# A masked row LSTM on one core: another deal of the input channels and gates, 32 products of 64 rows a half-step instead of 33, in an order of its own

## The chip, the cores and the metric

The kernel runs on one core of a Trainium2 chip. The time is that of the device for one execution, in microseconds (us), and less is better. The core has four engines that matter here: TensorE (PE) multiplies, and its weight loads are shown apart as PEld; VectorE (DVE), ScalarE (ACT) and GpSimd (POOL) work elementwise, and GpSimd sees only SBUF, not the PSUM banks into which TensorE writes. SyncE (SP) issues the DMAs. Each engine takes its instructions in the order of the program and waits on semaphores for the others.

## What is computed

The input x is 8 images of 96 channels, 128 rows and 128 pixels. It is normalised in 32 groups of channels. A convolution along the row (input to state, "is", three taps, masked) gives 384 gate channels for every pixel, and then a recurrence runs down the 128 rows. At each row a second convolution along the row (state to state, "ss", three taps) is taken of the last hidden row h, the two are added, and four gates f, i, o, g update the cell c and h. The sum of x and h is the output.

```python
m = np.ones((c_out, c_in, 1, kw), dtype=np.float32)
m[:, :, :, cx + 1:] = 0.0
m[:, :, 0, cx] = 0.0
m[:co, :ci, 0, cx] = 1.0
m[co:2 * co, :2 * ci, 0, cx] = 1.0
m[2 * co:3 * co, :, 0, cx] = 1.0
...
ss = lax.conv_general_dilated(h, W_ss, window_strides=(1,), padding=((1, 1),), dimension_numbers=('NCW', 'OIW', 'NCW')) + b_ss[None, :, None]
gates = ss + row_in
g5 = gates.reshape(B, 3, 4, Oc, Wd)
f = jax.nn.sigmoid(g5[:, :, 0].reshape(B, O, Wd))
i = jax.nn.sigmoid(g5[:, :, 1].reshape(B, O, Wd))
o = jax.nn.sigmoid(g5[:, :, 2].reshape(B, O, Wd))
g = jnp.tanh(g5[:, :, 3].reshape(B, O, Wd))
c_new = f * c + i * g
h_new = o * jnp.tanh(c_new)
```

The mask: the tap on the right is zero; the tap on the left is whole; of the centre tap the first third of the gate channels of each kind sees the first third of the input channels, the second third two thirds of them, and the last third sees all. All arithmetic is in fp32.

## The kernel before

**Tiles.** The 384 gate channels are three tiles of 128: A, B and C. Each is one PSUM bank of 128 x 512, in which the first 256 columns ("half 0") are for the even pixels and the last 256 for the odd ones ("half 1"), 4 images x 64 pixels each. A tile holds 96 channels of one gate (A: f, B: i, C: o) and 32 of g. The 8 images are two halves of 4 (s = 0, 1), whose recurrences are independent; they take turns. One row of one half is a **half-step** n, so there are 256, and place(n) tells the row and the half.

**Products.** The three taps of a pair of pixels are computed from four combinations (vs, the sum of the even and odd inputs; vf, their difference; vd, two shifted differences), with weights combined to match. A product is called by the weight it uses: "1" (vs, half 0), "2" (vf, half 1), "0" (vd, half 0), "3" (vd, half 1). Its 128 rows are 96 channels of h and 32 channels of x, which ride along in the same operand (normalise_shared puts x there). The other 64 channels of x have their own operands xs, of three parts, each held twice on rows 0 to 63 and 64 to 127, and products P, Q and E of 64 rows (half 0, half 1, half 0).

**Lanes.** The 128 rows of TensorE are used as two lanes of 64 rows, which run at once. In the regular part every product of 128 rows is issued as two of 64, one on each lane; P, Q and E need one lane only. In the order string a mark tells the lane: "<" rows 0 to 63, ">" rows 64 to 127; the second half of a product always takes the lane that the first didn't. That makes 24 products of 64 rows for h and 9 for xs, 33 a half-step. Two lanes must not write one bank at the same time, so HalfStep.mm keeps the last writer of each bank and, when the lane changes, has TensorE wait for its end (lines 489 to 491):

```python
before = self.writer.get(a)
if before is not None and before[0] != rows and whole not in (before[0], rows):
    lanes.wait(before[1])
```

lanes.wait drops a wait if one for the same or a later product has been made. The record of a bank's last writer is dropped at "even" below, when VectorE takes over.

**One half-step**, for a tile: products 1, 2, P and Q; "copy" (cp, ScalarE, L563) takes half 0 to SBUF with the bias; "even" (lo, VectorE, L567) adds copy and half 1 into half 0; "odd" (hi, L571) their difference into half 1; then products 0, 3 and E are added on top. Then tanh (ta, L575) and sigmoid (si, L587) on ScalarE, forget (fg, L592), gated (gt; the even pixels on GpSimd, L599, the odd ones on VectorE, L601), cell (ce, L611), cell_tanh (th, L616), output (ou, L624), which writes h into the operand tile hx of the next row. From hx come the sum (S, L637) and the difference (F, L641) on VectorE and the shifted differences (D, L645) on GpSimd. The residual (re, L662) adds h to x in place, and the rows are stored.

**Order.** The order of the engines' work in the regular part is written out by hand in the string PERIOD, which do(n, PERIOD, by_lanes=True) issues for every half-step n from 2 on. A name is an operation and a tile; a quote mark puts it to the half-step before (two marks, two before), "+" to the next, "*" to the one after; "a" and "b" are the even and odd pixels, "l" and "h" the first and last two images. W1, W2, W3 (widen, add_pixels, subtract_pixels: the xs of an image four rows ahead) and U (normalise_shared) are GpSimd's, X is the same on ScalarE. S, F and D are of the half-step two later than the name says. Before:

```python
PERIOD = (
    "1B> 3C'< D'' 2A> 0C'< 1A> siBa' 2B< 3C'> 1B< EC'> 2C< taA' 0C'> re'' 1C< fg' taB' PB+> "
    "PC+< cpA W1 loA cpB 1C> hiA loB hiB siBb' QCl+< taCa' taCb' EA< 2C> gtb' W2 3A< siC' "
    "0B> gta' 0A< cpC 3B> QA+< W3 cea' tha' EB> PA+< ceb' loC 0A> 0B< oua' thb' oub' X F' "
    "3A< 3B> QB*> S' 2A+< 2B+> 1A+< U QCh+> siA hiC"
)
```

**Other names.** hold() has a GpSimd instruction wait for a VectorE one that reads two SBUF operands: the shifted difference for the sum or difference before it, and the first of GpSimd's W or U after a residual for that residual. finish(n) and work(n) issue the loads (load, load_rows) and stores on SP's queue. In the first 150 us the statistics of the normalisation are taken while x streams in through the ring of buffers, first_rows copies the first rows out of PSUM, and the first half-steps run beside it, from the table of events. LAST is the order of the final half-steps.

Of the kernel before, what the change touches and what calls it, by code (L numbers as in the profile page):

```python
# [21 lines left out]
def kernel(  # L22
# [51 lines left out]
    O4 = 4 * C  # L74
    wl = const.tile([P, w.shape[1]], F32, name="wl")
# [3 lines left out]
    wh = const.tile([P, O4], F32, name="wh")  # L79
# [8 lines left out]
    wo = [wx[:, 0, :], wx[:, 1, :], tap[3]]  # L88

    def load_weights():  # L90
        nc.gpsimd.memset(pick, 0.0)
        nc.sync.dma_start(wl, w)
        for j in range(3):
            for lo, hi, shift in ((0, C, 0), (C, P, 2)):
                cols = slice(lo + (j + shift) % 3, hi, 3)
                nc.vector.tensor_scalar(
                    pick[:, j, cols], gm[:, 0, cols], quarter_of[:, j : j + 1], None, ALU.mult
                )
        for t in range(2):
            for half in range(2):  # L100
                nc.scalar.activation(
                    wt2[half * C2 : (half + 1) * C2, t], w_own[t * C2 : (t + 1) * C2], AF.Identity
                )

    def make_weights():

        for a in range(3):
            for j in range(4):
                third = a if j == 3 else j
                cols = bass.ds(a * P + j * 32, 32)  # L110
                if third < 2:
                    nc.gpsimd.memset(tap[0][C:P, cols], 0.0)
                if third < 1:
                    for h in range(2):
                        nc.gpsimd.memset(tap[4][h * C2 + 32 : (h + 1) * C2, cols], 0.0)
        nc.gpsimd.tensor_add(wm[:, 2, :], tap[1], tap[2])
# [6 lines left out]
        nc.gpsimd.tensor_scalar_mul(wh, tap[3], 0.5)  # L123
# [17 lines left out]
    cs = [const.tile([C, 2, BH, J], F32, tag=f"c{s}", name=f"c{s}") for s in range(NH)]  # L141
    for s in range(NH):
        nc.gpsimd.memset(xw[s][:, :, J : J + 1], 0.0)
        nc.gpsimd.memset(hx[s][0][0:C, 0], 0.0)
        for i in range(2):
            nc.gpsimd.memset(hx[s][i][:, :, 0, :, J : J + 1], 0.0)
            nc.gpsimd.memset(hx[s][i][:, :, 1, :, 0:1], 0.0)
# [9 lines left out]
    def load_rows(s, k, lo=0, hi=R):  # L157
        src = rows_of(s, k, 0, C2, lo, hi)
# [44 lines left out]
    def first_rows(b):  # L203
# [3 lines left out]
        for i in range(2):  # L207
            nc.scalar.activation(xr[s][i * C2 : (i + 1) * C2, j], first[b][0:C2], AF.Identity)
# [126 lines left out]
    def add_pixels(xw, n, total, engine=nc.gpsimd):  # L335

        engine.tensor_add(total, xw[:, 0:n, 0:J], xw[:, 0:n, J + 1 :])  # L337

    def subtract_pixels(xw, n, differences, engine=nc.gpsimd):

        engine.tensor_sub(  # L341
            differences,
            strided(xw[:, 0, :], 0, [(W + 1, n), (J, 2), (1, J)]),
            strided(xw[:, 0, :], J + 1, [(W + 1, n), (0, 2), (1, J)]),
# [13 lines left out]
    def own_row(xw, s, r, lo=0, hi=BH, engine=nc.gpsimd):  # L358
# [8 lines left out]
        )  # L367

# [25 lines left out]
    order = {"A": 0, "B": 1, "C": 2}  # L394

    def gt(n, s, row, shape=(C, 2 * HB)):
# [6 lines left out]
        "0": (0, 0, ("vd", 1)),  # L403
        "3": (1, 3, ("vd", 0)),
# [48 lines left out]
    residuals = []  # L453
# [3 lines left out]
    class HalfStep:  # L457


        def __init__(self, n):  # L460
            self.n, (self.row, self.s) = n, place(n)
            self.ps, self.m1, self.moving, self.done, self.gates, self.th = {}, {}, {}, set(), None, None
            self.started, self.images, self.halves, self.writer = set(), {}, {}, {}
            self.even_input = self.last = None
            self.hx = hx[self.s][self.row // R % 2][:, self.row % R]
            self.xs = xs[self.s][self.row // R % 2][:, self.row % R]
# [35 lines left out]
        def own(self, a, i):  # L502

            low = a == order["A"] or (a == order["C"] and (self.s == 0 or (self.n, i) == (1, 2)))
            rhs = self.xs[:, i].rearrange("p b j -> p (b j)")
            self.mm(a, i % 2, wo[i], rhs, slice(0, C2) if low else slice(C2, P))
# [24 lines left out]
        def t_(self, a):  # L531
# [5 lines left out]
            for half in range(2):  # L537
                self.mm(a, half, wh, rhs, rows)
# [34 lines left out]
        def tanh(self, a, lo=0, hi=BH, t=None):  # L573
            g, ps = self.g[a * 32 : (a + 1) * 32], self.ps[a][C:P]
            nc.scalar.activation(self.part(g, lo, hi, t), self.part(ps, lo, hi, t), AF.Tanh)  # L575


        def sigmoid(self, a, lo=0, hi=BH, t=None):
            if self.row == 0 and a == 0:
                return  # L580
            gate = self.part(self.ps[a][0:C], lo, hi, t)
            if t == 0 and NH < self.n < last:
# [4 lines left out]
            nc.scalar.activation(to, gate, AF.Sigmoid)  # L587

# [5 lines left out]
        def gated(self, lo=0, hi=BH, t=None):  # L594
            to = self.g if self.row > 0 else self.c
            to, i, g = (self.part(ap, lo, hi, t) for ap in (to, self.ps[1][0:C], self.g))
            if t == 0 and self.even_input is not None:
                i = self.even_input.rearrange("p (b j) -> p b j", b=BH)
                nc.gpsimd.tensor_mul(to, i, g)  # L599
# [34 lines left out]

        def total(self, engine=nc.vector, lo=0, hi=BH):
            e, o = self.pair(lo, hi)
            self.last = engine.tensor_add(self.operand("vs")[:, 0, lo:hi], e, o)  # L637

        def difference(self, engine=nc.vector, lo=0, hi=BH):
            e, o = self.pair(lo, hi)  # L640
            self.last = engine.tensor_sub(self.operand("vf")[:, 0, lo:hi], o, e)  # L641

        def shifted(self, lo=0, hi=BH):
            h = self.hx[:, 0, lo, :]
            diff = nc.gpsimd.tensor_sub(  # L645
                self.operand("vd", 2)[:, :, lo:hi],
                strided(h, 1, [(BH * JP - 1, 2), (JP, hi - lo), (1, J)]),
                strided(h, 0, [(BH * JP + 1, 2), (JP, hi - lo), (1, J)]),
            )
            hold(diff, self.last)  # L650

        def residual(self, lo=0, hi=BH, t=None):
# [8 lines left out]
            else:  # L661
                residuals.append(nc.vector.tensor_add(xo, xo, self.h))  # L662
# [28 lines left out]
    def beside(s, k, *images):  # L691
# [4 lines left out]
        (shared(0, 1, 0), own(0, 1, 3), [(load_rows, 0, 2)]),  # L696
# [3 lines left out]
        (shared(1, 1, 3), own(1, 1, 3), [(load_rows, 1, 2), (load, 0, 2)]),  # L700
# [5 lines left out]
    def work(n):  # L706
# [3 lines left out]
        if n < len(FIRST):  # L710
# [13 lines left out]
    def prepare(n, which="123"):  # L724
# [14 lines left out]
        for part, *args in now:  # L739
            made = part(*args)  # L740
            if made is not None and made.ins.engine == E.Pool and residuals:
                hold(made, residuals[-1])
                residuals.clear()
# [3 lines left out]
    def finish(n):  # L747
# [14 lines left out]
        "1B> 3C'< D'' 2A> 0C'< 1A> siBa' 2B< 3C'> 1B< EC'> 2C< taA' 0C'> re'' 1C< fg' taB' PB+> "  # L762
        "PC+< cpA W1 loA cpB 1C> hiA loB hiB siBb' QCl+< taCa' taCb' EA< 2C> gtb' W2 3A< siC' "
        "0B> gta' 0A< cpC 3B> QA+< W3 cea' tha' EB> PA+< ceb' loC 0A> 0B< oua' thb' oub' X F' "
        "3A< 3B> QB*> S' 2A+< 2B+> 1A+< U QCh+> siA hiC"
    )
    LAST = (
        "0C'' 3C'' EC'' siBa'' taA'' re''' taB'' taCa'' gta'' PB taCb'' siBb'' QC QB fg'' PA "
        "gtb'' cea'' QA PC siC'' tha'' ceb'' oua'' thb'' oub'' EA EB EC F'' S'' D'' re'' 1A "
        "2A 1B 1C 2B 2C cpA loA hiA cpB loB 3A hiB 0A 0B 3B cpC loC hiC 0C 3C taA siA fg taB "  # L770
        "siBa siBb taCa taCb gta gtb siC ceb cea thb tha oub oua rea reb"
# [17 lines left out]
    def do(n, names, by_lanes=False):  # L789

        for name in names.split():
# [22 lines left out]
            if part in ("S", "F", "D"):  # L814
# [21 lines left out]
        [x_pool.tile([P, CH], F32, tag=f"x{s}", name=f"xs{s}") for s in range(NH)]  # L836
        + [const.tile([P, CH], F32, tag=f"piece{i}", name=f"piece{i}") for i in range(2)]
        + [
            xs[s][1].rearrange("p r t b j -> p (r t b j)")[:, 0:CH]
            for s in range(NH)  # L840
        ]
    )
# [8 lines left out]
    def next_row():  # L851
        late[0].scale()
        late[0].shift()
        for j in range(BH - 1):
# [9 lines left out]
    def operands(n):  # L864
# [5 lines left out]
        step.done |= {"S", "F", "D"}  # L870
# [39 lines left out]
    def keep_warm(count):  # L910
        if not early_done and 1 not in steps:
# [31 lines left out]
            do(-2, "PA PB QA QB PC QC EA EB EC"),  # L943
# [16 lines left out]
        at(5, 7): lambda: (  # L960
            do(-2, "loA hiA"),
# [11 lines left out]
            do(-2, "taA"),  # L973
# [3 lines left out]
            do(-2, "taB"),  # L977
# [7 lines left out]
            do(-2, "siC"),  # L985
# [234 lines left out]
```

## Time and profile before

| | |
|---|---|
| time, median of 3 runs | 1965.98 us (1965.78 to 1966.8) |
| span of the profiled execution, first to last instruction | 1965.0 us |
| mean granted TensorE clock | 0.995 |
| chain of waits, TensorE's share | 94%, of which the products of line 492 93% |
| mean DMA rate | 119 GB/s |
| start, 0 to 150 us: PE, DVE, ACT busy | 92.84, 110.27, 99.64 us |
| end, 1940 to 1965 us: PE, DVE busy | 16.38, 16.11 us |

The profile shows one execution. A row of a timeline has the start and the duration in us, the engine, the line of the kernel, the operation, the output and inputs by name, partitions x elements, and in brackets how long the engine had been idle and what ended it; neighbours of one kind are drawn together ("x2"). The groups give busy time, mean duration in ns, and the idle time before them. One matmul instruction of fp32 shows as two records, its two passes. Engines off the chain may be idle without cost.

### The profile page before, as it was taken

Reading aid. Unit: us, or ns where it says so; the run is one execution under the profiler, and the core shown is the slowest. Engines: PE = TensorE matmul, PEld = TensorE weight load, DVE = VectorE, ACT = ScalarE, POOL = GpSimd, SP = SyncE. Lnnn points to the kernel's source line nnn. Section 1 sums busy time; section 2 is a strip of 40 time slices with the busy share of each in tenths; the row PEclk is TensorE's granted clock in tenths of the full one; section 3 lists DMA queues with packets and bytes.
Section 4 is the critical chain, followed back from the end, with each engine's and each line's share of the span. In section 5 each row is a group of like instructions: output and inputs, shape, how many; then the busy total and the mean of one; then the engine's idle time right before and its main releaser. Section 6 shows DMA issues by size and latency. Waiting matters only on the chain.

```text
span 1965.0 us, 46105 instructions
## 1 busy us (share of the span) xinstructions
PE 1899.2 (97%) x17416; PEld 1817.2 (92%) x17416; DVE 1798.8 (92%) x4015; ACT 1558.1 (79%) x3493; POOL 1354.2 (69%) x1645
## 2 busy tenths in 40 slices
PE   3689999999999999999999999999999999999998
PEld 0359999999999999999999999999999999999997
DVE  5888999999999999999999999999999999999997
ACT  6678788878888887887888788888888878888886
POOL 3347777777777777777777777777777777777751
PEclk9989999999999999999999999999999999999999
DMA  9994434544443454445345453534544443354411
GB/s 402 408 309 94 102 81 115 119 98 101 100 107 85 106 119 98 109 91 115 86 98 119 98 117 87 116 88 91 119 106 111 93 107 96 83 119 112 104 33 33
DMA packets 101277, 234.64 MB, mean 119 GB/s; under 512 B 5824, under 2 KB 7360, under 8 KB 95040
## 3 DMA queue, kind: packets, MB, share of 16 engines
q1 hardware_dynamic: 101056, 231.70, 45.8%
q8 instruction: 138, 2.26, 0.5%
q14 instruction: 83, 0.68, 0.1%
HBM read 181.34 MB, written 50.33 MB: 118 GB/s over the span
## 4 chain that ended last, share of the span: by engine, by line
PE 94%; DMA 3%; DVE 2%; ACT 1%; issue 0%; POOL 0%; SPq 0%; DVEq 0%; ACTq 0%
PE ps L492 93%; DMA xs<-in_x_dram 3%; DVE bst L1098 1%; PE pv L274 0%; PE rows L198 0%; ACT g L575 0%; PE rows L183 0%; ACT xs L239 0%; ACT ps L587 0%; SPq L1085 0%; DVE hx L624 0%; POOL xw L320 0%; PE dm L274 0%; ACT xs L240 0%; ACT L587 0%
## 5 line engine op out<-in xcount | busy, mean ns | idle before, releaser
L492 PE MATMUL ps<-vd,wl 64*128 64x256 f32 (+1 forms) x6080 | 1190.4, 376 | 2.8 <-DVE ps L571 2.7
L492 PEld LDWEIGHTS ps<-vd,wl 64*128 64x128 f32 (+1 forms) x6080 | 871.1, 186 | 21.9 <-issue 3.5
L492 PE MATMUL ps<-vs,wm 64*128 64x256 f32 (+1 forms) x3046 | 821.5, 377 | 0.7 <-DVE vs L637 0.7
L492 PE MATMUL ps<-vf,wm 64*128 64x256 f32 (+1 forms) x3046 | 765.5, 377 | 0.0
L492 PE MATMUL ps<-xs,wx 64*128 64x128 f32 (+1 forms) x3582 | 747.7, 349 | 1.8 <-POOL xs L337 1.7
L492 PEld LDWEIGHTS ps<-xs,wx 64*128 64x128 f32 x3582 | 605.7, 188 | 7.1 <-POOL xs L337 3.3
L587 ACT ACTIVATE ps<-ps 96x512 f32<-96x512 f32 (+1 forms) x768 | 388.2, 506 | 232.3 <-PE ps L492 223.8
L492 PEld LDWEIGHTS ps<-vs,wm 64*128 64x128 f32 (+1 forms) x3046 | 529.3, 187 | 12.6 <-issue 1.6
L575 ACT ACTIVATE g<-ps 32x256 f32<-32x256 f32 (+1 forms) x1021 | 468.2, 481 | 19.3 <-PE ps L492 0.6
L492 PEld LDWEIGHTS ps<-vf,wm 64*128 64x128 f32 (+1 forms) x3046 | 461.9, 186 | 18.1 <-DVE vf L641 1.0
L492 PE MATMUL ps<-xs,wt 64*128 64x256 f32 x1518 | 449.3, 377 | 0.0
L563 ACT ACTIVATE m<-ps,wl 128x256 f32<-128x256 f32 x766 | 362.3, 473 | 106.6 <-PE ps L492 81.4
L645 POOL TENSOR_TENSOR vd<-hx 128x512 f32<-128x512 f32 x257 | 288.0, 1121 | 179.9 <-DVE vs L637 171.8
L567 DVE TENSOR_TENSOR ps<-m,ps 128x256 f32<-128x256 f32 x768 | 324.1, 422 | 79.4 <-ACT m L563 79.2
L571 DVE TENSOR_TENSOR ps<-m,ps 128x256 f32<-128x256 f32 x768 | 327.4, 427 | 17.7
L662 DVE TENSOR_TENSOR x<-x,hx 96x512 f32<-96x512 f32 x253 | 339.3, 1341 | 0.0
L320 POOL TENSOR_SCALAR xw<-xr,rstd,nmr 128x512 f32<-128x512 f32 (+1 forms) x267 | 209.2, 785 | 131.7 <-DVE x L662 114.1
L320 POOL TENSOR_SCALAR hx<-x,rstd,nmr 32x512 f32<-32x512 f32 (+1 forms) x245 | 219.4, 895 | 75.2 <-POOL xs L341 53.6
L341 POOL TENSOR_TENSOR xs<-xw 128x512 f32<-128x512 f32 (+1 forms) x254 | 269.8, 1062 | 0.0
L492 PEld LDWEIGHTS ps<-xs,wt 64*128 64x128 f32 x1518 | 264.8, 187 | 0.9 <-issue 0.3
L599 POOL TENSOR_TENSOR g<-i,g 96x256 f32<-96x256 f32 x251 | 181.9, 725 | 120.6 <-ACT g L575 112.7
L616 ACT ACTIVATE th<-c 96x256 f32<-96x256 f32 (+1 forms) x509 | 191.0, 418 | 2.4 <-DVE c L611 2.1
(101 smaller groups left out, 1487.4 us busy)
## 6 DMA issues: line engine op xcount, KB each, us to landing
xr<-in_x_dram SPq DMA_DIRECT2D x124, 512.0 KB, 6.9
x<-in_x_dram SPq DMA_DIRECT2D x62, 768.0 KB, 8.6
out_dram<-x SPq DMA_DIRECT2D x62, 768.0 KB, 5.0
xs<-in_x_dram SPq DMA_DIRECT2D x31, 1024.0 KB, 10.8
piece<-in_x_dram SPq DMA_DIRECT2D x16, 1024.0 KB, 11.0
x<-in_x_dram SPq DMA_DIRECT2D x62, 256.0 KB, 6.3
out_dram<-x SPq DMA_DIRECT2D x2, 576.0 KB, 3.7
xs<-in_x_dram SPq DMA_DIRECT2D x2, 512.0 KB, 9.7
```

The source lines that it names most:

```text
L320: return engine.tensor_scalar(dst, src, scale, shift, ALU.mult, ALU.add)
L341: engine.tensor_sub(differences, strided(xw[:, 0, :], 0, [(W + 1, n), (J, 2), (1, J)]), strided(xw[:, 0, :], J + 1, [(W + 1, n), (0, 2), ( ...
L492: made = nc.tensor.matmul(self.ps[a][:, bass.ts(half, HB)][:, cols], weights[rows, bass.ts(a, P)], rhs[rows, cols], start=new, stop=False, ...
L563: nc.scalar.activation(self.m1[a], m1, AF.Identity, bias=column)
L567: nc.vector.tensor_add(self.ps[a][:, 0:HB], self.m1[a], self.ps[a][:, HB:])
L571: nc.vector.tensor_sub(hi, self.m1[a], hi)
L575: nc.scalar.activation(self.part(g, lo, hi, t), self.part(ps, lo, hi, t), AF.Tanh)
L587: nc.scalar.activation(to, gate, AF.Sigmoid)
L599: nc.gpsimd.tensor_mul(to, i, g)
L616: nc.scalar.activation(self.part(self.th, lo, hi, t), self.part(self.c, lo, hi, t), AF.Tanh)
L645: diff = nc.gpsimd.tensor_sub(self.operand("vd", 2)[:, :, lo:hi], strided(h, 1, [(BH * JP - 1, 2), (JP, hi - lo), (1, J)]), strided(h, 0, ...
L662: residuals.append(nc.vector.tensor_add(xo, xo, self.h))
```

## The change

The gate channels are dealt to the tiles by the thirds of the mask. A holds f and the last third of o; B holds i and the last third of g; C holds the first two thirds of o and of g. The 32 channels of x that ride along with h are now the first third, and xs holds the other two. With this deal tile C, whose gates are of the first two thirds only, needs of the third part of xs only the 32 channels of the second third; these ride on rows 96 to 127 of a new operand te (called ve in the products), in the product "3". So product E of tile C goes: 32 products of 64 rows. Q is whole, no longer in two halves, and E writes half 1.

The shifted difference splits: shifted_even (D0) writes te's first 96 rows, shifted_odd (D1) the operand vo of 128 rows. Rows 96 to 127 of te are a copy of rows 64 to 95 of xs's third part, made by a DMA, spare, on SP's queue, and at the start by ScalarE (spare_rows). The last third of the output gate is a sigmoid of its own (o2), from A's bank to C's. Tile A has no tanh any more. GpSimd is held behind sums and differences as well as residuals, whichever GpSimd instruction comes next (after_reads). first_rows copies in four pieces instead of two; the ring has other buffers; the order strings are new.

```diff
-    wh = const.tile([P, O4], F32, name="wh")
+    wh = const.tile([P, 2, 2 * P], F32, name="wh")
...
-    wo = [wx[:, 0, :], wx[:, 1, :], tap[3]]
+    wo = [wx[:, 0, :], wx[:, 1, :], tap[4]]
...
+    te = [const.tile([P, 2, R, BH * J], F32, tag=f"te{s}", name=f"te{s}") for s in range(NH)]
...
-        src = rows_of(s, k, 0, C2, lo, hi)
+        src = rows_of(s, k, 32, C, lo, hi)
...
-        nc.sync.dma_start(flat[C:P], rows_of(s, k, C2, C))
+        nc.sync.dma_start(flat[C:P], rows_of(s, k, 0, 32))
...
-        for i in range(2):
-            nc.scalar.activation(xr[s][i * C2 : (i + 1) * C2, j], first[b][0:C2], AF.Identity)
+        for i in range(4):
+            of = 32 + i % 2 * 32
+            nc.scalar.activation(
+                xr[s][i * 32 : (i + 1) * 32, j], first[b][of : of + 32], AF.Identity
+            )
...
+    def spare_of(s, i, r0, r1, lo=0, hi=BH):
+
+        return (
+            te[s][C:P, i, r0:r1].rearrange("p r (b j) -> p r b j", b=BH)[:, :, lo:hi],
+            xs[s][i][C2 : C2 + 32, r0:r1, 2, lo:hi],
+        )
...
+    def spare(s, k, r0=0, r1=R):
+        nc.sync.dma_start(*spare_of(s, k % 2, r0, r1))
...
-        "0": (0, 0, ("vd", 1)),
-        "3": (1, 3, ("vd", 0)),
+        "0": (0, 0, ("vo", 0)),
+        "3": (1, 3, ("ve", 0)),
...
+    def after_reads(made):
+
+        if both_sbuf and made is not None and made.ins.engine == E.Pool:
+            hold(made, both_sbuf[-1])
+            both_sbuf.clear()
...
-                self.mm(a, i % 2, wo[i], self.xs[:, i].rearrange("p b j -> p (b j)"), rows)
+                self.mm(a, min(i, 1), wo[i], self.xs[:, i].rearrange("p b j -> p (b j)"), rows)
...
+        def last_output_gate(self):
+            nc.scalar.activation(self.ps[2][C2:C], self.ps[0][C:P], AF.Sigmoid)
...
-                nc.gpsimd.tensor_mul(to, i, g)
+                after_reads(nc.gpsimd.tensor_mul(to, i, g))
...
-            self.last = engine.tensor_add(self.operand("vs")[:, 0, lo:hi], e, o)
+            self.reads(engine.tensor_add(self.operand("vs")[:, 0, lo:hi], e, o))
...
+        def shifted_even(self, lo=0, hi=BH):
+            if self.row > 0:
+                h, to = self.hx[0:C, 0, lo:hi], self.moving["ve"][0:C, 0]
+                to = to.rearrange("p (b j) -> p b j", b=BH)[:, lo:hi]
+                after_reads(nc.gpsimd.tensor_sub(to, h[:, :, 1 : J + 1], h[:, :, 0:J]))
+
+        def shifted_odd(self, lo=0, hi=BH):
+            h, to = self.hx[:, 1, lo:hi], self.operand("vo")[:, 0, lo:hi]
+            after_reads(nc.gpsimd.tensor_sub(to, h[:, :, 0:J], h[:, :, 1 : J + 1]))
+
         def shifted(self, lo=0, hi=BH):
-            h = self.hx[:, 0, lo, :]
-            diff = nc.gpsimd.tensor_sub(
-                self.operand("vd", 2)[:, :, lo:hi],
-                strided(h, 1, [(BH * JP - 1, 2), (JP, hi - lo), (1, J)]),
-                strided(h, 0, [(BH * JP + 1, 2), (JP, hi - lo), (1, J)]),
-            )
-            hold(diff, self.last)
+            self.shifted_even(lo, hi)
+            self.shifted_odd(lo, hi)
...
-            ([(load_rows, s, k + 2)] + ([(load, 0, k + 2)] if s == 1 else [])
-             if r == R - 2 and k + 2 < NB else [])
-            + ([LATER[n]] if n in LATER else []),
+            ([LATER[n]] if n in LATER else [])
+            + ([(spare, s, k + 1)] if r == R - 2 and k + 1 < NB else [])
+            + ([(load_rows, s, k + 2)] + ([(load, 0, k + 2)] if s == 1 else [])
+               if r == R - 2 and k + 2 < NB else []),
...
     PERIOD = (
+        "2B> hiC' 3C'< 2A> taB' 0C'< fg' re'' D1'' U 1A> cpA loA 1B< 3C'> hiA 2B< cpB 0C'> taCa' "
+        "gta' 1C< W2 taCb' QB+> 2C< PC+> loB siC' PB+< hiB 2C> 0A< o2' 1C> W3 gtb' EA< QC+> cpC "
+        "cea' 0B< ceb' 3A> tha' thb' 3B< PA+> EB< loC 0A> oua' oub' X S' QA+< F' 3B> 3A< 0B> W1+ "
+        "1A+< 1B+> siA siBb 2A+< siBa D0'"
     )
...
     perm = np.concatenate(
-        [np.concatenate([idx[:, a].reshape(-1), idx[a, 3]]) for a in range(3)]
+        [idx[third, gate] for third, gate in (
+            (0, 0), (1, 0), (2, 0), (2, 2), (0, 1), (1, 1), (2, 1), (2, 3),
+            (0, 2), (1, 2), (0, 3), (1, 3),
+        )]
     )
```

More of the change, by code (lines that the diff above doesn't have):

```diff
@@ L74 @@
     O4 = 4 * C
+    order = {"A": 0, "B": 1, "C": 2}
     wl = const.tile([P, w.shape[1]], F32, name="wl")
@@ L537, in t_ @@
             for half in range(2):
-                self.mm(a, half, wh, rhs, rows)
+                self.mm(a, half, wh[:, half], rhs, rows)
         def whole(self, kind, a):
@@ L580, in sigmoid @@
                 return
-            gate = self.part(self.ps[a][0:C], lo, hi, t)
-            if t == 0 and NH < self.n < last:
+            gate = self.part(self.ps[a][0 : C2 if a == order["C"] else C], lo, hi, t)
+            if a == order["B"] and t == 0 and NH < self.n < last:
                 self.even_input = self.tile("i", (C, HB))
@@ L695 @@
         ([], own(0, 1, 1), own(0, 1, 2)),
-        (shared(0, 1, 0), own(0, 1, 3), [(load_rows, 0, 2)]),
+        (shared(0, 1, 0), own(0, 1, 3), [(spare, 0, 1), (load_rows, 0, 2)]),
         (beside(0, 1, 1) + shared(0, 1, 2), own(1, 1, 0), []),
@@ L699 @@
         (beside(1, 1, 1) + shared(1, 1, 2), own(1, 1, 2), []),
-        (shared(1, 1, 3), own(1, 1, 3), [(load_rows, 1, 2), (load, 0, 2)]),
+        (shared(1, 1, 3), own(1, 1, 3), [(spare, 1, 1), (load_rows, 1, 2), (load, 0, 2)]),
         (shared(0, 2, *SHARED[0]), own(0, 2, 0), []),
@@ L739, in prepare @@
         for part, *args in now:
[L740 to L743, printed above, removed]
+            after_reads(part(*args))
     closed = set()
@@ L869, in operands @@
         step.shifted()
-        step.done |= {"S", "F", "D"}
+        step.done |= {"S", "F", "D0", "D1"}
     def row_of(s, r):
```

130 lines of the change are left out of this document (76 added, 54 removed), and 3 rows, old and new, of the table PARTS.

## The prediction

> **What bounds the kernel now.** The page comes first.
>
> ```profile
> span 1965.0 us, 46105 instructions
> PE 1899.2 (97%) x17416; PEld 1817.2 (92%) x17416; DVE 1798.8 (92%) x4015; ACT 1558.1 (79%) x3493; POOL 1354.2 (69%) x1645
> PE 94%; DMA 3%; DVE 2%; ACT 1%; issue 0%; POOL 0%; SPq 0%; DVEq 0%; ACTq 0%
> ```
>
> TensorE fills the chain of waits. The windows view over the regular part has it busy in every microsecond; its columns are length, then PE, PEld, DVE, ACT and POOL busy with counts, then clock, DMA share and GB/s.
>
> ```profile
> 300.00:1900.00 1600.00, 1600.00 (x15263) 1567.71 (x15260) 1498.21 (x3367) 1291.64 (x2975) 1164.08 (x1342) 1.00 0.44 101
> ```
>
> A busy TensorE is not yet a full one, for two lanes of 64 rows work at once and one may idle under the other. So I read one half-step in the timeline, VectorE first (start, duration, operation).
>
> ```profile
> 999.90 0.43 DVE L567 TENSOR_TENSOR ps<-m,ps 128x256 f32<-128x256 f32 x1 [0.57 <-ACT m L563]
> ...
> 1001.49 0.41 DVE L601 TENSOR_TENSOR g<-ps,g 96x256 f32<-96x256 f32 x1
> 1001.91 0.75 DVE L611 TENSOR_TENSOR c<-ps,g 96x256 f32<-96x256 f32 x2
> ...
> 1003.69 0.42 DVE L641 TENSOR_TENSOR vf<-hx 128x256 f32<-128x256 f32 x1
> 1004.03 0.42 DVE L637 TENSOR_TENSOR vs<-hx 128x256 f32<-128x256 f32 x1
> ...
> 1004.70 1.51 DVE L662 TENSOR_TENSOR x<-x,hx 96x512 f32<-96x512 f32 x1
> ...
> 1007.03 0.43 DVE L567 TENSOR_TENSOR ps<-m,ps 128x256 f32<-128x256 f32 x1 [0.21 <-ACT m L563]
> ```
>
> From the first "even" (L567) to the next is 1007.03 - 999.90 = 7.13 us: the half-step. It holds 33 products on two lanes, 16.5 slots, so a slot is 7.13 / 16.5 = 0.432 us. A product is two matmul passes, so a pass takes 0.216 and starts on the two lanes together come every 0.108. Were a lane idle, the slots would not add up to the half-step. The kernel is bound by the number of products, with nothing left over.
>
> How it gets there shows where the program order makes one lane wait for the other, at 3C'> behind 0C'< (both read vd, in the bank of tile C):
>
> ```profile
> 1005.57 0.38 PE L492 MATMUL ps<-vd,wl 64*128 64x256 f32 x1
> 1005.57 0.19 PEld L492 LDWEIGHTS ps<-vd,wl 64*128 64x128 f32 x1
> ...
> 1005.78 0.38 PE L492 MATMUL ps<-vd,wl 64*128 64x256 f32 x1
> ...
> 1006.22 0.18 PEld L492 LDWEIGHTS ps<-vd,wl 64*128 64x128 f32 x1
> ...
> 1006.32 0.38 PE L492 MATMUL ps<-vd,wl 64*128 64x256 f32 x1
> ```
>
> The pass at 1005.78 is the second of 0C'<; its weights were loaded 0.21 us ahead, at 1005.57. It ends at 1006.16. The load of 3C'> starts 0.06 after that and its matmul 0.10 after the load, with the other loads' lead of 0.21 gone. So from the start of a product to the earliest useful start of a product on the other lane in the same bank: 0.216 + 0.38 + 0.06 + 0.10, about 0.755 us. And 1005.57 to 1006.32 is just that: here the wait costs nothing, by a hair.
>
> **The change, part by part.** *Products.* The third product of tile C goes, and QC, cut in two halves, becomes whole: 32 whole products, 16 slots, 16 x 0.432 = 6.91 us. That alone is -0.22 us a half-step. How many half-steps, from the groups by form:
>
> ```profile
> L492 PE MATMUL ps<-vs,wm 64*128 64x256 f32 x3012 | 810.3, 376 | 0.1
> L645 POOL TENSOR_TENSOR vd<-hx 128x512 f32<-128x512 f32 x255 | 286.8, 1125 | 179.9 <-DVE vs L637 171.8 <-DVE ps L571 2.2 <-PE ps L492 0.4
> L599 POOL TENSOR_TENSOR g<-i,g 96x256 f32<-96x256 f32 x251 | 181.9, 725 | 120.6 <-ACT g L575 112.7 <-DVE ps L567 7.9
> L337 POOL TENSOR_TENSOR xs<-xw 128x256 f32<-128x256 f32 x252 | 161.7, 642 | 20.9
> L341 POOL TENSOR_TENSOR xs<-xw 128x512 f32<-128x512 f32 x252 | 268.5, 1066 | 0.0
> L575 ACT ACTIVATE g<-ps 32x512 f32<-32x512 f32 x515 | 304.7, 592 | 13.1 <-PE ps L492 0.6
> L587 ACT ACTIVATE ps<-ps 96x512 f32<-96x512 f32 x513 | 294.5, 574 | 232.2 <-PE ps L492 223.8
> ```
>
> vs feeds 6 products of two passes in each: 3012 / 12 = 251 half-steps. 251 x 0.22 = 55 us would come off.
>
> *The order.* This is where I part from that sum. Number the products of the new PERIOD 1 (2B>) to 32 (2A+<). The marks alternate strictly: odd ones take the upper lane, even ones the lower, which starts 0.108 behind. Line 490's rule makes a product wait for the last one in its bank when that was on the other lane. In the new string this happens three places apart eight times. From an even to an odd product three places is 2 x 0.432 - 0.108 = 0.756 us: enough for 0.755, as in the row above. That holds for 4 to 7 (tile C), 12 to 15 (C), 18 to 21 (A), 24 to 27 (B) and 32 to 3 (A). From an odd to an even one it is 0.432 + 0.108 = 0.540: 0.215 short. That is 11 to 14 (QB+>, PB+<), 23 to 26 (PA+>, QA+<) and 25 to 28 (0A>, 3A<). The old order has waits three places apart too, but its half products QCl and QCh, half a slot each, change which lane leads in mid-period, and PA, QA and PB, QB share lanes there. The new string has nothing of the kind, so a lane has to be stalled to change the lead, and the other lane to change it back.
>
> Followed round: 3 to 11 is 4 slots on one lane; 11 to 14 a wait; 14 to 18 is 2 slots; 18 to 21 a wait; 21 to 23 is 1; 23 to 26 a wait; 26 to 32 is 3; 32 to the next 3 a wait. 10 x 0.432 + 4 x 0.755 = 4.32 + 3.02 = **7.34 us**, against 7.13 now. (25 to 28 and 24 to 27 come out even on the way.) That is +0.21 x 251 = +53 us.
>
> The price of a wait is measured where it just fits; when late, the load is not hidden either. A sum came late once early in the run:
>
> ```profile
> 227.29 0.18 PEld L492 LDWEIGHTS ps<-vs,wm 64*128 64x128 f32 x1 [0.41 <-DVE vs L637]
> ...
> 227.30 0.48 PE L492 MATMUL ps<-vs,wm 64*128 64x256 f32 x1
> ...
> 227.62 0.39 PE L492 MATMUL ps<-vs,wm 64*128 64x256 f32 x2
> ```
>
> The late product starts with its load, but its second pass comes 0.32 after the first, not 0.216: again 0.10 for the load. So 0.755 stands from both sides, within 0.01 by the rounding of the rows: 4 x 0.01 x 251 = 10 us either way.
>
> The Trainium skill, TensorE: Matmul & The Clock Gate, Part 3, The mechanism, says that the PE pulls a weight load for a non-conflicting row group ahead of matmuls in flight. If that held past the wait, the 0.10 would fall away and the round would take about 4.32 + 4 x 0.65 = 6.92 us. The load at 1005.57 with its lead of 0.21 agrees with the rule; the one at 1006.22, right behind the end that it waits for, shows that it does not reach past a wait, and I go by that row.
>
> *VectorE* keeps its instructions. From "even" to the end of the sum it needs 1004.45 - 999.90 = 4.55 us; with S now ahead of F 0.34 less, 4.21. In a round of 7.34 the sum is ready some 0.2 us before 1A+< can start, so this chain does not bind. Tile A's tanh goes and o2 comes, 32x512 each (592 ns); C's sigmoid on 64 partitions instead of 96 costs the same, as the rows of 32 and 96 partitions do. ScalarE: 0.
>
> *GpSimd.* One difference of 1.125 us becomes two, each between 642 and 725 ns: +0.24 us on an engine that is 1164 / 1600 = 73% busy; 0, as long as TensorE binds. The new holds put W1 behind F and D1 behind the residual; behind them wait U, the gated product and W2, and for the gated product the cell. Before, the residual and the difference met on VectorE's account (1.51 us above); now W1 and D0 run while VectorE does "odd" and forget, and VectorE has 102 us of 1600 idle as it is.
>
> *Queues and start.* spare adds a copy of 128 KB on SP's queue every fourth row of each half, ahead of load_rows. It is issued in the half-step after row R - 2 and read three half-steps (over 20 us) on.
>
> ```profile
> x<-in_x_dram SPq DMA_DIRECT2D x62, 256.0 KB, 6.3
> 135.12 1.18 ACT L208 ACTIVATE xr<-rows 64x512 f32<-64x512 f32 x2
> 138.98 0.17 ACT L1119 ACTIVATE minus<-dm 128x2 f32<-128x2 f32 x1 [2.68 <-PE dm L274]
> ```
>
> Twice that size lands in 6.3 us: 0. first_rows doubles its two copies, +1.18 us; behind the last one ScalarE sits idle for 2.68 us: 0, and +1.2 without that cover.
>
> The sum: 1965.0 + 53 = 2018 of span, and 1.0 us lies around the span (median 1965.98 less 1965.0): **2019 us**.
>
> **The rivals.** *The waits cost nothing* and the product count sets the time: 1966 - 55 = 1911 us. For it: the lanes are separate, and the lower could drift behind until its waits fit. Against: a wait from even to odd holds the upper lane back by what the lower one lags, and 32 to 3 has 0.001 us of room. It needs loads to pass a wait, which the row at 1006.22 denies. 13%.
>
> *The waits are hidden but the recurrence binds.* 1A+< to 1A> takes 3.5 slots and 0.108 (1.62 us), its first pass, its second (at 1006.11) and the start of the copy 0.216 + 0.38 + 0.03 = 0.63, copy to "even" 0.51 (1006.52 to 1007.03), VectorE 4.21, load and start 0.16:
>
> ```profile
> 1006.11 0.38 PE L492 MATMUL ps<-vs,wm 64*128 64x256 f32 x1
> ...
> 1006.52 1.01 ACT L563 ACTIVATE m<-ps,wl 128x256 f32<-128x256 f32 x2 [0.29 <-PE ps L492]
> ```
>
> together 7.13; without the wait of the cell for GpSimd (1001.91 - 1001.49 is 0.42, and two cells start 0.35 apart) 7.06: 1948 us. It needs the same hidden waits. 8%.
>
> *One round of lead changes instead of two*: 6.91 + 0.216 = 7.13, 1966 us, no difference. It would take a wait that the program drops because a later product was already waited for; I find none of the eight so covered. 5%.
>
> *GpSimd in the way of VectorE as well.* If W3 (1.07 us) still reads when the sum S is ready, S waits, as the residual does at 1004.70. From 0.2 us of overlap on, each further 0.1 us adds 25: 2044 and more. By the rows above GpSimd has some 5.5 us of work in a round of 7.34, so it should be done in time. 6%.
>
> **How the numbers follow.** The forecast has 68%: 2019 us, on its own 2005 to 2032 (10 us for the price of the wait, some for fill and drain). 1911 and more than 2032 are 19%, so the range is 1935 to 2032. A measurement tells 0.2%, 4 us, from no change. Faster is 13 + 8 = 21%, the same 5%, slower 68 + 6 = 74%.
>
> **What would show it.** The half-step by VectorE's "even" should be 7.34 us, and a window of 1600 us should hold 64 / 7.34 x 1600, about 13950 matmuls instead of 15263, with TensorE still busy throughout, since the lanes stall in turn. In the timeline the loads of PB+<, 3A>, QA+< and 2A> should start 0.06 us behind the end of a product of the other lane, and PB+< and QA+< some 0.2 us after their own lane fell free. 7.06 with loads right behind the sum would mean the recurrence; 6.91 that the waits are free. Wrong, too, if a product here turns out not to take 0.432 us.

## The result, and the profile after

The changed kernel takes 2088.65 us (2088.27 to 2091.67, four runs) against 1965.88 us beside it: 1.0627 times as long, with a 95% interval of 1.0612 to 1.0643. The forecast was 2019 us, with a range up to 2032. The direction was right; the time is 70 us past the forecast and 57 us past the range.

The page of the changed kernel, its span, its busy times and its chain:

```profile
span 2086.5 us, 45382 instructions
PE 2014.3 (97%) x16396; PEld 1787.4 (86%) x16396; DVE 1736.6 (83%) x4015; ACT 1605.3 (77%) x3516; POOL 1384.8 (66%) x1917
PE 92%; DMA 2%; DVE 2%; ACT 2%; POOL 1%; issue 0%; SPq 0%; DVEq 0%; ACTq 0%; POOLq 0%
```

Read this way, TensorE still bounds the kernel. The same window of 1600 us says otherwise:

```profile
300.00:1900.00 1600.00, 1600.00 (x13474) 1449.85 (x13471) 1354.58 (x3159) 1239.71 (x2789) 1116.82 (x1473) 1.00 0.40 101
```

13474 matmuls instead of 15263. A half-step now has 32 products of two passes, 64 matmuls, so it takes 1600 x 64 / 13474 = 7.60 us, not the 6.91 of its products and not the 7.34 of the forecast. TensorE is "busy" in all 1600 us because one lane works while the other stands. (7.60 - 7.13) x 251 = 118 us of the 121.5 by which the span grew: nearly all of it is in the regular part.

The groups by form tell where a new wait is (busy, mean ns, then the idle time ahead of the group and what ended it):

```profile
L653 DVE TENSOR_TENSOR c<-ps,g 96x256 f32<-96x256 f32 x506 | 190.3, 416 | 119.9 <-ACT ps L629 119.9
```

VectorE's cell (L653) waits 119.9 us in all for line 629, which is o2, the new sigmoid of the last third of the output gate. One round in the timeline, on the way from one sum to the next:

```profile
1004.37 1.01 ACT L602 ACTIVATE m<-ps,wl 128x256 f32<-128x256 f32 x2 [0.27 <-PE ps L531]
...
1004.88 0.43 DVE L606 TENSOR_TENSOR ps<-m,ps 128x256 f32<-128x256 f32 x1 [0.46 <-ACT m L602]
...
1006.17 0.72 POOL L641 TENSOR_TENSOR g<-i,g 96x256 f32<-96x256 f32 x1
...
1006.47 0.41 DVE L643 TENSOR_TENSOR g<-ps,g 96x256 f32<-96x256 f32 x1
...
1006.69 0.57 ACT L629 ACTIVATE ps<-ps 32x512 f32<-32x512 f32 x1
...
1007.28 0.47 ACT L602 ACTIVATE m<-ps,wl 128x256 f32<-128x256 f32 x1
...
1007.36 0.75 DVE L653 TENSOR_TENSOR c<-ps,g 96x256 f32<-96x256 f32 x2 [0.47 <-ACT ps L629]
...
1007.82 0.75 ACT L658 ACTIVATE th<-c 96x256 f32<-96x256 f32 x2
...
1009.14 0.42 DVE L683 TENSOR_TENSOR vs<-hx 128x256 f32<-128x256 f32 x1
...
1009.62 0.30 PEld L531 LDWEIGHTS ps<-vs,wm 64*128 64x128 f32 x4 [0.29 <-DVE vs L683]
1009.62 0.70 PE L531 MATMUL ps<-vs,wm 64*128 64x256 f32 x4
...
1011.97 1.01 ACT L602 ACTIVATE m<-ps,wl 128x256 f32<-128x256 f32 x2 [0.33 <-PE ps L531]
```

The cell's own inputs are there early: the odd gated product starts at 1006.47, the even one ends at 1006.89 on GpSimd. But o2 ends at 1007.26, and the cell starts 0.10 later. The distances add up to the round: copy to even 0.51, even to odd gated product 1.59, that to the cell 0.89 (before it was 0.42), cell to sum 1.78, sum to the first load that needs it 0.48, load to the next copy 2.35: 7.60. The load stands 0.06 behind the sum's end (1009.14 + 0.42), and its matmul starts with it, so TensorE waits for VectorE here, not the other way round. The distance from sum to load alone does not tell this. In the kernel before, the load was just as close behind the sum, which ended at 1004.45 in the round that the forecast read:

```profile
1004.50 0.18 PEld L492 LDWEIGHTS ps<-vs,wm 64*128 64x128 f32 x1
...
1004.71 0.38 PE L492 MATMUL ps<-vs,wm 64*128 64x256 f32 x1
```

There the matmul came its usual 0.21 behind the load, and no time was lost. So the way from sum to sum had little to spare in the 7.13 us of the kernel before: about 0.1 us, by an estimate from these rows, the lead of 0.21 less the 0.10 that a late load costs. In the window from 300 to 1900 us the first matmul has that lead in every half-step of the kernel before, and starts with its load in every one of the changed kernel.

Why should the cell wait for o2? o2 reads rows 96 to 127 of ps[0], tile A's bank, and writes to ps[2]; the cell reads rows 0 to 95 of ps[0]. Of what o2 reads and the cell reads, they share no element, only the bank.

### The profile page after: what moved, and what is told of

It reads as the page before. It is cut to its first block, busy times and chain, and to the rows that moved or that the text cites. A ratio compares the mean times of both kernels' runs of the same rounds, so it can differ in the third digit from the quotient of the medians.

```text
span 2086.5 us, 45382 instructions
## 1 busy us (share of the span) xinstructions
PE 2014.3 (97%) x16396; PEld 1787.4 (86%) x16396; DVE 1736.6 (83%) x4015; ACT 1605.3 (77%) x3516; POOL 1384.8 (66%) x1917
## 4 chain that ended last, share of the span: by engine, by line
PE 92%; DMA 2%; DVE 2%; ACT 2%; POOL 1%; issue 0%; SPq 0%; DVEq 0%; ACTq 0%; POOLq 0%
PE ps L531 92%; DMA xs<-in_x_dram 1%; DMA te<-in_x_dram 1%; DVE bst L1154 1%; ACT g L615 0%; ACT ps L626 0%; POOL xw L337 0%; DVE hx L666 0%; DVE c L653 0%; ACT m L602 0%; DVE vs L683 0%; PE rows L212 0%; ACT ps L629 0%; ACT th L658 0%; PE pv L291 0%
## 5 line engine op out<-in xcount | busy, mean ns | idle before, releaser
L531 PE MATMUL ps<-vo,wl 64*128 64x256 f32 (+1 forms) x3040 | 900.5, 376 | 2.1 <-DVE ps L610 1.9
L531 PE MATMUL ps<-xs,wx 64*128 64x256 f32 (+1 forms) x3080 | 822.6, 394 | 2.0 <-POOL xs L354 1.8
L531 PE MATMUL ps<-te,wl 64*128 64x256 f32 (+1 forms) x3040 | 750.8, 391 | 0.1
L531 PE MATMUL ps<-vs,wm 64*128 64x256 f32 (+1 forms) x3046 | 661.5, 394 | 8.0 <-POOL vs L683 5.2
L626 ACT ACTIVATE ps<-ps 64x512 f32<-64x512 f32 (+2 forms) x768 | 362.5, 499 | 271.6 <-PE ps L531 263.3
L531 PEld LDWEIGHTS ps<-vo,wl 64*128 64x128 f32 (+1 forms) x3040 | 549.7, 186 | 21.2 <-DVE ps L610 4.7
L531 PEld LDWEIGHTS ps<-te,wl 64*128 64x128 f32 (+1 forms) x3040 | 422.1, 185 | 58.8 <-PE ps L531 0.5
L615 ACT ACTIVATE g<-ps 32x512 f32<-32x512 f32 x765 | 317.7, 447 | 11.4 <-PE ps L531 2.0
L653 DVE TENSOR_TENSOR c<-ps,g 96x256 f32<-96x256 f32 (+1 forms) x507 | 190.9, 416 | 120.0 <-ACT ps L629 119.9
L697 POOL TENSOR_TENSOR vo<-hx 128x256 f32<-128x256 f32 x257 | 157.2, 612 | 177.3 <-DVE x L713 167.2
```

Source lines behind the costliest of these rows:

```text
L531: made = nc.tensor.matmul(self.ps[a][:, bass.ts(half, HB)][:, cols], weights[rows, bass.ts(a, P)], rhs[rows, cols], start=new, stop=False, ...
L653: nc.vector.tensor_add(c, f, g)
L697: after_reads(nc.gpsimd.tensor_sub(to, h[:, :, 0:J], h[:, :, 1 : J + 1]))
```

## The experiments

Two theories. **R**: the way from sum to sum sets the half-step, through the cell's wait for o2. **L**: the lane waits set it, as forecast, only dearer. In the table "lane waits" means that three of the four lane waits are gone, and "cell's wait" that the cell no longer waits for o2. The ratio is to the kernel before, measured beside each run. The half-step is 1600 x 64 over the matmuls in the window from 300 to 1900 us.

| run | what is gone or moved in the changed kernel | us | ratio to before, 95% | matmuls | half-step |
|---|---|---|---|---|---|
| (changed) | | 2088.65 | 1.0612 to 1.0643 | 13474 | 7.60 |
| e2_lanes | lane waits | 2089.32 | 1.0621 to 1.0653 | 13471 | 7.60 |
| e10_wait_alone | cell's wait | 2046.68 | 1.0400 to 1.0431 | 13789 | 7.43 |
| e1_o2_first | o2 earlier | 2045.83 | 1.0404 to 1.0435 | 13790 | 7.43 |
| e4_no_o2 | no o2 | 2045.25 | 1.0397 to 1.0432 | 13789 | 7.43 |
| e6_other_bank | lane waits, o2 on another bank | 2031.77 | 1.0323 to 1.0354 | 13901 | 7.37 |
| e9_other_rows | lane waits, cell's wait | 2030.12 | 1.0315 to 1.0349 | 13900 | 7.37 |
| e3_both | lane waits, o2 earlier | 2003.38 | 1.0180 to 1.0214 | 14119 | 7.25 |
| e7_sum_first | e3 and 1A> ahead of 2A> | 2002.64 | 1.0176 to 1.0206 | 14120 | 7.25 |
| e8_copy_late | e7 and tile C's copy later | 1990.10 | 1.0112 to 1.0142 | 14239 | 7.19 |
| e5_no_o2_lanes | lane waits, no o2 | 1971.19 | 1.0024 to 1.0054 | 14361 | 7.13 |

**The lanes alone.**

```diff
-2C< PC+> loB siC' PB+< hiB 2C>
+2C< PB+> loB siC' PC+< hiB 2C>
...
-3B< PA+> EB< loC 0A> oua'
+3B< 0A> PA+< loC EB> oua'
```

> Products of TensorE change places so that no product follows one of the other lane in the same bank by three places on the dear side (PB+> ahead of PC+<, 0A> ahead of PA+<): three of the four lane waits of a half-step lose their cause. Theory R: the way from sum to sum has the same products on it as before, 7.60 us, 2088 us within 5 us. Theory L: the half-step falls by 0.21 us for each wait that goes, to 6.91 to 7.13 us, 1910 to 1970 us.

Not a microsecond came back: 2089.32 us. The four lane waits that the forecast had found are in the changed kernel's trace, and three of them can go without effect. L falls as the cause of 7.60.

**o2 ahead of tile C's sigmoid.** In PERIOD, nothing else:

```diff
-PC+> loB siC' PB+< hiB 2C> 0A< o2' 1C>
+PC+> loB o2' PB+< hiB 2C> 0A< siC' 1C>
```

> The last third's sigmoid (ScalarE, ps[0] to ps[2]) and tile C's sigmoid change places in ScalarE's order; nothing else. Theory R (the cell, which reads ps[0], waits for that sigmoid, and the way from one sum to the next sets the half-step of 7.60 us): the sigmoid then ends some 0.6 us earlier, VectorE's cell starts when GpSimd's product is there, at 0.03 behind its end, 0.44 earlier than now; but the copy of tile C still stands ahead of the cell's tanh on ScalarE and holds it at 0.38 behind its own start, so that of the 0.44 only some 0.16 comes through: half-step 7.44 us, time about 2050 us. Theory L (the four waits between lanes set the half-step, each some 0.07 us dearer than the forecast had it): nothing moves on TensorE, 7.60 us and 2088 us.

2045.83 us. The groups by form of this run:

```profile
L653 DVE TENSOR_TENSOR c<-ps,g 96x256 f32<-96x256 f32 x506 | 187.8, 410 | 2.2 <-ACT ps L629 1.5 <-POOL g L641 0.5
```

The cell's 119.9 us of waiting are 2.2. As R says. But that the time fits R's 2050 us is luck: R had ScalarE's row set it, and the lanes do, as the next run shows.

**o2 left out.** The output gate of the last 32 channels is then another value.

```diff
-hiB 2C> 0A< o2' 1C>
+hiB 2C> 0A< 1C>
```

> The last third's sigmoid is left out of the regular half-steps (the output gate of the last 32 channels is then a wrong value); the products and their lanes stay as in the changed kernel. Theory R: the cell waits for GpSimd alone (0.44 us earlier) and ScalarE loses an instruction of 0.57 us, so the way from sum to sum falls to about 7.16 us; the lane waits then bind at the forecast's 7.34 us: about 2019 us. Theory L with dearer waits: 7.60 us, 2088 us.

2045.25 us and 7.43 us a half-step, as in the run above (13789 and 13790 matmuls), though ScalarE has 0.57 us less to do. Neither 7.34 nor 7.60: with the cell's wait gone the lanes are the bound, and they cost 0.09 more than forecast. The passes that start right behind the other lane (0.48 long) give the round, from one such half-step. By the numbers of the prediction they belong to the products 14 at 1000.86 (the last of an "x3"), 21 at 1002.48, 26 at 1003.67, 3 at 1005.78, the next 14 at 1008.32. The pieces are 1.62, 1.19, 2.11 and 2.54, together 7.46 (other half-steps have 7.40, the mean is 7.43); the forecast has 1.62, 1.19, 2.05 and 2.48. The price of a wait is right to 0.01. What it lacks is 0.06 in pieces where no wait should be felt. TensorE's timeline at these places:

```profile
1000.64 0.70 PE L531 MATMUL ps<-xs,wx 64*128 64x256 f32 x3
...
1002.48 0.81 PE L531 MATMUL ps<-te,wl 64*128 64x256 f32 x4
...
1005.78 0.48 PE L531 MATMUL ps<-vf,wm 64*128 64x256 f32 x1
...
1008.10 0.70 PE L531 MATMUL ps<-xs,wx 64*128 64x256 f32 x3
```

The view of the line that issues the lane waits, and the timeline in the third piece:

```profile
L466 PEldq EVENT_SEMAPHORE  x375: 51/51/51, 161.5 to 2021.0; - x188
```

```profile
1003.67 0.48 PE L531 MATMUL ps<-xs,wx 64*128 64x256 f32 x1
...
1003.99 0.38 PE L531 MATMUL ps<-xs,wx 64*128 64x256 f32 x1
1004.10 0.55 PE L531 MATMUL ps<-te,wl 64*128 64x256 f32 x2
...
1004.48 0.38 PE L531 MATMUL ps<-te,wl 64*128 64x256 f32 x1
```

Most lane waits ride on the weight load: there are eight a half-step, but only 375 instructions in all are of that line. Those are waits that stand alone (51 ns; one is at 1004.08). It is satisfied at once, but the loads behind it come late: the pass that starts at 1004.20 (the second of the "x2") has its weights 0.04 ahead instead of 0.21, lasts 0.44 instead of 0.38, and the next on its lane starts 0.28 later instead of 0.216. In the window there are 323 passes of 0.44 to 0.45 us, each within 0.25 us behind such a wait: 1.5 a half-step, 1.5 x 0.06 = 0.09. This was read from the trace and not tried by itself.

**Both away.** o2' left out (as above) and the lanes of the first run.

> Both: the last third's sigmoid left out of the regular half-steps (a wrong output gate for the last 32 channels) and the products in the order without the three lane waits. Theory R: what is left is the way from sum to sum, 7.16 us, about 1975 us. Theory L: 6.91 to 7.13 us as with the new order of products alone, 1910 to 1970 us, and no better than that run. If both sigmoid and lanes cost the half-step in sum, this run is below either alone by what the other took away.

1971.19 us, 7.13 us: below either alone. This is the way from sum to sum without o2; the forecast's rival had worked out 7.06 to 7.13 for it from the kernel before. The half-steps are not all alike here: some take 7.04 to 7.06, more take 7.15 to 7.18, where those of e3, e6 and e9 agree within 0.01. In all of them, short or long, the first matmul starts with its load, right behind the sum, as in the changed kernel. What lengthens the longer ones stays open.

**Both, with o2 kept.**

> Both edits that keep the result: the last third's sigmoid ahead of tile C's, and the products in the order without the three lane waits. The runs so far: the first edit alone 7.43 us a half-step, the second alone 7.60, the second with the sigmoid left out 7.09. Theory R: with the lanes out of the way the way from sum to sum sets the time, and on it ScalarE's row from tile A's copy to the cell's tanh, which without that sigmoid took 2.96 us and with it 0.54 + 0.50 + 0.28 + 0.40 + 0.59 + 0.60 + 0.38 = 3.29 us: 7.09 + 0.33 = 7.42 us, about 2045 us, no better than the first edit alone. Theory L: 7.09 us or less, 1971 us.

2003.38 us, 7.25. Below o2 moved alone (7.43), which R had not expected: there the lanes had bound. R's number, 7.42, was 0.17 too high. ScalarE's row was taken 0.12 too long; from tile A's copy to the tanh it is

```profile
1002.83 1.01 ACT L602 ACTIVATE m<-ps,wl 128x256 f32<-128x256 f32 x2 [0.48 <-PE ps L531]
1003.87 0.65 ACT L615 ACTIVATE g<-ps 64x256 f32<-64x256 f32 x2
1004.55 0.57 ACT L629 ACTIVATE ps<-ps 32x512 f32<-32x512 f32 x1
1005.15 0.57 ACT L626 ACTIVATE ps<-ps 64x512 f32<-64x512 f32 x1
1005.64 0.46 ACT L602 ACTIVATE m<-ps,wl 128x256 f32<-128x256 f32 x1
1006.00 0.71 ACT L658 ACTIVATE th<-c 96x256 f32<-96x256 f32 x2
```

1006.00 - 1002.83 = 3.17 us, not 3.29: 0.21 more than the 2.96 without o2. The rest is the 7.09 from which R started: with the short half-steps of the run before, 7.04 + 0.21 = 7.25. That sum was made after the run and is not shown by one of its own. In the changed kernel the row is 1007.82 - 1004.37 = 3.45.

**The wait by itself**, first by another bank. The instruction stays where it is on ScalarE, with its size, and reads ps[2] (the gate of the last 32 channels is another value); the products as in the first run.

```diff
-            nc.scalar.activation(self.ps[2][C2:C], self.ps[0][C:P], AF.Sigmoid)
+            of = self.ps[2][C2:C] if 0 < self.n < last else self.ps[0][C:P]
+            nc.scalar.activation(self.ps[2][C2:C], of, AF.Sigmoid)
```

> The second edit alone (2089 us, 7.60 us) with ScalarE's and VectorE's orders as they are, and the last third's sigmoid reads ps[2], which it writes, instead of ps[0] (a wrong output gate for the last 32 channels): the same instruction of the same size at the same place on ScalarE. If it is the cell's wait for that sigmoid on bank ps[0] that costs, the cell starts 0.44 us earlier and the half-step falls to about 7.42 us (2045 us), the rest being ScalarE's row. If it is only that ScalarE has one more instruction ahead of the cell's tanh, nothing changes: 7.60 us, 2089 us.

2031.77 us, 7.37 against 7.60 with the same orders on all engines (R had put it at 7.42). So 0.23 us a half-step come from the shared bank. Then with the bank kept, and only the cell's wait not made (self.o2 is o2's instruction), in the order of the first run and in the changed kernel's own:

```diff
-                nc.vector.tensor_add(c, f, g)
+                made = nc.vector.tensor_add(c, f, g)
+                if self.o2 is not None:
+                    tc.declare_no_dep(
+                        made.ins, self.o2, reason="rows 0 to 95 here, rows 96 to 127 there"
+                    )
```

> The products in the order without the three lane waits (2089 us so far, 7.60 us a half-step), everything else as in the changed kernel, and the cell is declared independent of the last third's sigmoid: the one reads rows 0 to 95 of bank ps[0], the other rows 96 to 127. No instruction moves and the result is the reference's. If the wait put in for the shared bank is what the cell loses: the same as with the sigmoid on another bank, 7.37 us, about 2032 us. If the two engines then hinder each other in the bank, more than that, up to 2089 us.

> The changed kernel with nothing but that wait away. Theory R with the lanes as second bound: the way from sum to sum falls to 7.37 us, and the lane waits, which took 7.43 us with the sigmoid moved and with it left out, bind: 7.43 us, about 2045 us. If lane waits and the cell's wait add up rather than stand side by side: more than 2045 us.

2030.12 and 2046.68 us: both as expected, within 2 us. In the timeline of e9_other_rows the two instructions run at once (o2 is L629, the cell L654):

```profile
1004.60 0.41 DVE L644 TENSOR_TENSOR g<-ps,g 96x256 f32<-96x256 f32 x1
...
1004.82 0.57 ACT L629 ACTIVATE ps<-ps 32x512 f32<-32x512 f32 x1
1004.93 0.74 DVE L654 TENSOR_TENSOR c<-ps,g 96x256 f32<-96x256 f32 x2
...
1005.41 0.47 ACT L602 ACTIVATE m<-ps,wl 128x256 f32<-128x256 f32 x1
...
1005.78 0.71 ACT L663 ACTIVATE th<-c 96x256 f32<-96x256 f32 x2
```

The cell starts 0.33 behind the odd gated product, with o2 still in the bank until 1005.39; they overlap so in every half-step of the window (217 of 217), and neither gets longer by it (o2 0.57 us, the cell 0.41 on average, as in the changed kernel). The tanh now stands 0.37 behind tile C's copy: ScalarE's row is next. The Trainium skill, PSUM — Partial Sum Buffer, PSUM bank collisions raise a hardware error, says that two engines may not use the same 32 rows of a bank at once, while different groups of 32 rows of it may be used together, and calls a guard by whole bank the simple version. The rows above agree, and price the simple version: 0.23 us a half-step with the lanes mended, 0.17 without.

**Further.** Two tries to get below the kernel before, on top of e3_both. First 1A> and 2A> change places:

```diff
-3C'< 2A> taB' 0C'< fg' re'' D1'' U 1A> cpA
+3C'< 1A> taB' 0C'< fg' re'' D1'' U 2A> cpA
```

> Both edits, and 1A> changes places with 2A>: the two products that tile A's copy waits for then stand five places apart in the row instead of seven... counted in products, the copy's last product comes two places (0.43 us) earlier, and 2A>, which VectorE's sum of tile A needs 0.5 us later, takes its place. Theory R: the way from sum to sum loses 0.42 us (ScalarE's tanh of tile B then holds the copy): 7.42 - 0.42 = 7.00 us; TensorE's 32 products take 6.91 us and 0.06 us more for each satisfied wait that stands as an instruction of its own: about 7.00 us, 1945 us, less than before. If the way from sum to sum is not what binds: as with both edits alone.

2002.64 us, the same as with both edits alone, and not the 1945 us that R expected.

```profile
1003.01 0.38 PE L531 MATMUL ps<-vf,wm 64*128 64x256 f32 x1
...
1003.43 1.02 ACT L602 ACTIVATE m<-ps,wl 128x256 f32<-128x256 f32 x2 [0.47 <-PE ps L531]
```

The copy starts at 1003.43 in this run's round, 0.04 behind the end of the last pass of 2A> (1003.01 + 0.38), which writes the half that the copy does not read. So it waits for the whole bank, and which of the two halves comes last does not matter. Then tile C's copy behind the tanh:

```diff
-2B> hiC' 3C'< 1A> taB' 0C'<
+2B> hiC' 0C'< 1A> taB' 3C'<
...
-EA< QC+> cpC cea' 0B< ceb' 3A> tha' thb' 3B< 0A> PA+< loC EB>
+EA< QC+> cea' 0B< ceb' 3A> tha' thb' cpC 3B< 0A> PA+< EB>
...
-QA+< F' 3B>
+QA+< F' loC 3B>
```

> As the run before, and tile C's copy moves on ScalarE from ahead of the cell's tanh to behind it, with VectorE's even of tile C behind the difference and 0C< ahead of 3C<. Theory R: the row from tile A's copy to the tanh falls by another 0.33 us, so the way from sum to sum is near 6.7 us and TensorE alone binds: 6.91 us and the satisfied waits, 6.93 to 7.00 us, 1925 to 1945 us. If VectorE's odd of tile C, now 0.34 us later, holds 3C< back, the gain is given back: 7.0 to 7.1 us.

1990.10 us, a gain of 12, and above both numbers expected. The rows point to a reason:

```profile
1003.43 0.42 DVE L606 TENSOR_TENSOR ps<-m,ps 128x256 f32<-128x256 f32 x1
...
1003.88 0.43 DVE L610 TENSOR_TENSOR ps<-m,ps 128x256 f32<-128x256 f32 x1
...
1004.37 0.18 PEld L531 LDWEIGHTS ps<-vo,wl 64*128 64x128 f32 x1
...
1006.40 0.47 ACT L602 ACTIVATE m<-ps,wl 128x256 f32<-128x256 f32 x1 [0.29 <-PE ps L531]
```

The load of 0C'< at 1004.37 stands 0.06 behind the end of "odd" (1003.88 + 0.43), though 0C'< needs "even" alone: again the bank, as it seems. 2B< comes later for it, and tile B's copy (1006.40) idles 0.29 for TensorE. No run took this wait away, so its share of the time is not shown. No version here beats the kernel before; its 7.13 us is where this order of products ended even without o2.

## Why the prediction was wrong

- **The step that failed**: "VectorE keeps its instructions ... so this chain does not bind", with "ScalarE: 0". The count of instructions was right; but o2 takes the place of tile A's tanh only in the count. The tanh stood far ahead of the cell (taA' before fg' in the old string); o2 stands between tile C's sigmoid and copy, in ScalarE's row from tile A's copy to the cell's tanh, and shares its bank with the cell that comes next. Together that put 0.47 us on the way from sum to sum: 7.13 became 7.60, which is +118 us. The runs without the three lane waits divide it. Without o2 the way is 7.13 (e5); with o2, but without the cell's wait, 7.37 (e9); with both, 7.60 (e2). So 0.24 us are o2's place in ScalarE's row, and 0.23 the cell's wait. The forecast had asked what the new instruction costs, not what stands behind it and who waits for it.
- **The lane waits**: where they would be, right, all four. Their price, 0.755, right to 0.01. Their sum, 7.34, too small by 0.09 (e1, e4 and e10: 7.43), because a satisfied wait was taken as free. With that term the forecast would be 2019 + 23 = 2042, and e10, the change without the cell's wait, takes 2046.68. So the mechanism was real, but a second, longer one lay over it: without three of its lane waits the kernel takes as long as with them. That the forecast had the direction right is therefore not its own mechanism at work in the changed kernel, though e10 shows that it would have sufficed.
- **"The waits are hidden but the recurrence binds"** came nearest in kind, and e5's 7.13 without o2 is at the end of its 7.06 to 7.13. It too left o2 out.
- **"The waits cost nothing", 1911 us**, and 6.91 us a half-step: no run came near; the lowest mean half-step is 7.13 (e5). In e4's round the four passes that the lane waits hold back are 0.48 long, with their load behind the wait, as the forecast took from the row at 1006.22.
- **GpSimd: 0.** Right: in the changed kernel the cell's idle time has no GpSimd in it. The rival with GpSimd in the way, 2044 us and more, fits the time, but not these rows.
- **Start, queues, DMA: 0.** Right within the 3.5 us of span that the half-steps leave over.
- **The signs to look for** served: 13474 matmuls and 7.60 us fitted none of the cases, which said at once that something was left out. "Loads right behind the sum", named as the mark of the recurrence, were there, but they were there in the kernel before as well; the mark that tells the two apart is the matmul that starts with its load.

## What to carry to other kernels

An instruction that replaces another of the same size adds nothing to its engine's work and may still put most of its length on the chain (0.47 us of o2's 0.57 here): ask what stands behind it in its engine's order, and list which banks it touches, who else touches them, and where it stands against them in time. Rows that don't overlap are no protection where waits are made by the bank. And when two bounds lie near one another (7.43 and 7.60 here), mending the shorter one shows nothing (e2), and mending the longer one shows only the gap between them (e10, 0.17); take both away, each alone and together.

## What the hardware showed that was not expected

A satisfied wait on TensorE's queue that rides on a weight load takes no time that the trace shows: in e4's round the load at 1002.80 carries one, and its pass at 1003.02 has its lead of 0.21 and is 0.38 long. When the wait is an instruction of its own, at a place where the lane has no slack, the pass is 0.06 longer: the window of e4 has 323 such waits and 323 passes of 0.44 to 0.45 us. In e2, where TensorE stands still for the sum, 369 such waits come with only 158 such passes. No run changed these waits alone.
